# Both expert stages of a cross-attention and mixture-of-experts block: rows sorted by expert into 128-row blocks in place of every row through every expert

## The chip, the cores and the metric

The kernel runs on one core of one Trainium2 chip. The metric is device time in microseconds of that core, from the first to the last instruction and what lies around it. All arithmetic is in fp32.

## What is computed

There are 32 sequences of 56 rows of width 256, and for each a context of 1500 rows. Four stages follow each other, each added to the residual: a decayed sum of the context, 16 experts of which each row takes the best 6, attention over the masked context, and 2 experts of which each row takes the better. The reference computes every expert for every row and weights the results, zero where an expert is not chosen:

```python
# layer 0: E = 16, K = 6, MOE_D = 176
scores = jax.nn.softmax(logits.astype(jnp.float32), axis=-1)
topk_w, topk_idx = jax.lax.top_k(scores, K)
cw = cw.at[jnp.arange(T)[:, None], topk_idx].add(topk_w)
for e in range(E):
    g = h @ w_gate[e].T
    u = h @ w_up[e].T
    out = jax.nn.silu(g) * u @ w_down[e].T
    y = y + cw[:, e:e + 1].astype(x.dtype) * out
# layer 1: E = 2, FF = 1024
sel = jnp.argmax(probs, axis=-1)
...
out = jnp.einsum('etd,te->td', y, onehot * top_w)

x = x + _L0_xattn_ref(_layernorm(x, axis=-1), ctx_2048, ...)
x = x + _L0_ffn_ref(_layernorm(x, axis=-1), ...)
x = x + _L1_xattn_ref(_layernorm(x, axis=-1), ctx_2048, mask_BxS2_bk0)
x = x + _L1_ffn_ref(_layernorm(x, axis=-1), ...)
```

## The kernel before

The residual `xr` stays in SBUF as 16 tiles. A tile holds a pair of sequences, one in partitions 0 to 55, the other in 64 to 119. Four tiles are a group, and a group has 448 real rows.

The first stage streams the context through four buffers with DMAs issued by SP (`load_ctx`, L93 and L96) and adds it up on PE (L205). The layer-0 weights are loaded between these (L200). Then the small matmuls of the decayed sum follow (L239 to L273), and VectorE normalizes and adds.

The first expert stage goes over the four groups. `route0` normalizes a group, transposes it (L342), computes the gate (L357), picks the best six with `V.max` and `V.match_replace` (L403, L407), and writes the weights to DRAM, from where SP reads them back, spread over the partitions (L383, L422). `experts` takes 22 chunks of 128 hidden units. In each, the weights are the stationary operand and the group's 448 transposed rows move through the array: four matmuls for gate and up (L302), a silu on ScalarE (L307), two multiplications on VectorE (L308, L310), and two matmuls down (L315). The down matmuls of a chunk come after the gate matmuls of the next. The group ahead is routed while a group is in `experts`. `add_back` turns the result (L330) and adds it (L334), and the rows of the attention are normalized and transposed into `xnp`.

The attention goes over the 16 tiles: transposes of the context (L477), scores (L514), softmax (L530), transposes of the probabilities (L541), and their product with the context (L555). The mask is prepared on POOL (L497), and the layer-1 weights are loaded by three DMAs from POOL's queue (L458). The second expert stage has the same form as the first, with 16 chunks, and each group's output goes out by SP (L616).

The Tile framework puts in the semaphores, and its scheduler sets the order of each engine's instructions by the program's order and the buffers that are free.

Of the kernel before, what the change touches and what calls it, by code (L numbers as in the profile page):

```python
# [8 lines left out]
F32 = mybir.dt.float32  # L9
U8 = mybir.dt.uint8  # L10
AF = mybir.ActivationFunctionType
ALU = mybir.AluOpType
# [4 lines left out]
P = 128  # L17
B, S, D, T = 32, 56, 256, 1500
KD = D // P  # halves of the model width
NP = B // 2  # pairs of sequences: rows 0..55 and 64..119 of a tile  # L20
GP = 4  # pairs in a group
NG = NP // GP
TOK = 2 * S  # tokens of a pair
GT = GP * TOK  # tokens of a group
TA = 11  # context rows t = 11 p + j of the first 1408, then 92 more
# [4 lines left out]
NF0 = E0 * F0 // P  # L30
E1, F1 = 2, 1024
NF1 = E1 * F1 // P
EPS = 1e-5
BIG = 1e30
ISC = 1.0 / 16.0  # 1 / sqrt(D)
# [3 lines left out]
def xattn_ffn_kernel(  # L39
# [27 lines left out]
    rows = ctx.enter_context(tc.tile_pool(name="rows", bufs=2))  # L67
    cpool = ctx.enter_context(tc.tile_pool(name="ctx", bufs=4))
    dram = ctx.enter_context(tc.tile_pool(name="scratch", bufs=1, space=DRAM))

# [1 line left out]
    ident = const.tile([P, P], F32, name="ident")  # L72
    make_identity(nc, ident)
    flip = const.tile([P, P], F32, name="flip")  # ones where row + column = 127
    G.memset(flip, 0.0)
    G.affine_select(
        out=flip, in_=flip, compare_op=ALU.not_equal, fill=1.0,
        base=-(P - 1), pattern=[[1, P]], channel_multiplier=1,
    )
    ones = const.tile([P, P], F32, name="ones")  # L80
    G.memset(ones, 1.0)
    eps = const.tile([P, 1], F32, name="eps")
    G.memset(eps, EPS)

# [4 lines left out]
    xnp = const.tile([P, KD, NP * P], F32, name="xnp")  # normed, transposed, with pad columns  # L89
# [12 lines left out]
    def norm_scales(src, n):  # L102
        """Mean and 1 / sqrt(var + eps) of each row of n tiles."""
# [19 lines left out]
    with tc.tile_pool(name="w0", bufs=1) as w0p:  # L123
        wg0_sb = w0p.tile([P, KD, E0 * F0], F32, name="wg0_sb")
        wu0_sb = w0p.tile([P, KD, E0 * F0], F32, name="wu0_sb")
        wd0_sb = w0p.tile([P, NF0, D], F32, name="wd0_sb")
        with tc.tile_pool(name="p1", bufs=1) as p1, tc.tile_pool(
            name="p1_ps", bufs=2, space=PSUM
        ) as ps, tc.tile_pool(name="p1_acc", bufs=1, space=PSUM) as psa:
            kd = p1.tile([1, 4], F32, name="kd")  # L130
            nc.sync.dma_start(out=kd[:, 0:1], in_=decay)
            # row u of the context counts sum_{j < T - u} k^j times in the sum of the states
            # k = sigmoid(decay) by exp(-|decay|), which stays finite
# [32 lines left out]
            # count columns at place B - 1 of a row of zeros  # L166
# [25 lines left out]
            # four column groups of the array, each with a quarter of the chunks  # L192
            acc = psa.tile([P, D], F32, name="acc")
            ncq = NCH // 4
            w0_after = {12: (wg0_sb, wg0), 18: (wu0_sb, wu0), 24: (wd0_sb, wd0)}
            for b in range(B):
                c = load_ctx(b)
                if b in w0_after:
                    sb, w = w0_after[b]
                    nc.sync.dma_start(out=sb, in_=w)  # L200
# [12 lines left out]
            xn0 = p1.tile([P, NP, D], F32, name="xn0")  # L213
# [8 lines left out]
            selb = p1.tile([B, B, 64], F32, name="selb")  # L222
            V.tensor_copy(selb, ident[0:B, 0:B].unsqueeze(2).to_broadcast([B, B, 64]))
            selbf = selb.rearrange("q b s -> q (b s)")
# [44 lines left out]
            for g in range(NG):  # L269
                gs = slice(GP * g, GP * g + GP)  # L270
                for p in range(GP * g, GP * g + GP):
                    bp = ps.tile([P, 512], F32, tag="ps", name="bp")
                    PE.matmul(  # L273
                        bp[:, 0:D], lhsT=selbf[:, p * P : (p + 1) * P], rhs=m_sb,
                        start=True, stop=True,
                    )
                    V.tensor_tensor(xn0[:, p, :], xn0[:, p, :], bp[:, 0:D], ALU.add)
# [5 lines left out]
        # the first two pairs of the cross attention load during the experts  # L283
# [393 lines left out]
```

## Time and profile before

| | |
|---|---|
| time, median of two runs | 1326.16 us (1325.67 to 1326.65) |
| span of the profiled execution | 1323.2 us |
| PE busy | 1160.0 us (88%), 5104 instructions |
| VectorE, ScalarE, POOL busy | 452.5, 250.5 and 70.4 us |
| expert matmuls, lines 302 and 315 | 258.0 + 254.9 + 254.3 us of PE |
| bytes moved | 143.79 MB, mean 109 GB/s |

The profile is of one execution. PE is the matmul engine and PEld its weight loads, which overlap it. DVE is VectorE, ACT is ScalarE, POOL is GpSimd, SP issues DMAs. An fp32 matmul leaves two records in the trace. A group of instructions is named by its line, its engine and output<-input. The runs' median lies 3 us above the profiled execution's span; no time other than the span is known for that execution.

### The profile page before, as it was taken

What the parts mean: (1) busy time and instruction counts of PE and PEld (TensorE: products, weight loads), DVE (VectorE), ACT (ScalarE), POOL (GpSimd) and SP (SyncE); (2) the same over time, 40 slices, a digit from 0 to 9 for tenths busy, and PEclk for the clock granted to TensorE, in tenths of its full rate; (3) what the DMA queues carried; (4) which work ended last, traced back from release to release, by engine and by line L of the source; (5) the groups of instructions that cost most, each with busy time, mean ns of one, the idle gap of its engine ahead of it and who ended that gap; (6) DMA issues with size and microseconds to landing.
All of it is one profiled execution on the core that took longest, in us unless ns stands there. A gap on an engine that the chain in (4) does not pass through costs nothing. (4 is left out here: it accounts for less than half of the span.)

```text
span 1323.2 us, 13044 instructions
## 1 busy us (share of the span) xinstructions
PE 1160.0 (88%) x5104; PEld 623.1 (47%) x5104; DVE 452.5 (34%) x1166; ACT 250.5 (19%) x412; POOL 70.4 (5%) x81
## 2 busy tenths in 40 slices
PE   5534455899999999999999998989898999999998
PEld 3111122455555555555445555656564545555554
DVE  2400008622532442332343443433434323232322
ACT  0000000211311321121143332323322111121111
POOL 1300002100000000000021011010100000000000
PEclk9576775799999999999999999999999999999999
DMA  9999990111111111111055345352520001000000
GB/s 304 332 340 338 346 321 35 49 65 56 42 50 51 47 50 49 49 53 53 18 204 198 145 154 185 113 189 108 192 94 15 15 0 28 0 28 1 14 0 14
DMA packets 38445, 143.79 MB, mean 109 GB/s; under 512 B 5031, under 2 KB 29168, under 8 KB 29424
## 3 DMA queue, kind: packets, MB, share of 16 engines
q1 hardware_dynamic: 35122, 134.03, 28.9%
q0 software_dynamic: 432, 6.29, 1.2%
q10 hardware_dynamic: 2830, 2.64, 0.8%
q8 instruction: 40, 0.66, 0.2%
q14 instruction: 21, 0.17, 0.0%
HBM read 140.98 MB, written 1.96 MB: 108 GB/s over the span
## 5 line engine op out<-in xcount | busy, mean ns | idle before, releaser
L302 PE MATMUL gp<-xnT,wg_sb 128*128 128x448 f32 x608 | 258.0, 543 | 0.0
L302 PE MATMUL up<-xnT,wu_sb 128*128 128x448 f32 x608 | 254.9, 540 | 0.0
L315 PE MATMUL y<-hh,wd_sb 128*128 128x448 f32 x608 | 254.3, 541 | 0.0
L308 DVE TENSOR_TENSOR sg<-sg,up 128x448 f32<-128x448 f32 x152 | 94.2, 620 | 422.0 <-PE up L302 417.3
L307 ACT ACTIVATE sg<-gp 128x448 f32<-128x448 f32 x152 | 82.3, 543 | 525.5 <-PE gp L302 517.8
L315 PEld LDWEIGHTS y<-hh,wd_sb 128*128 128x128 f32 x608 | 114.0, 190 | 112.4 <-issue 105.4
L302 PEld LDWEIGHTS up<-xnT,wu_sb 128*128 128x128 f32 x608 | 114.4, 191 | 106.7 <-issue 106.7
L205 PE MATMUL acc<-ctx,cz 128*32 128x256 f32 (+1 forms) x768 | 82.3, 562 | 93.7 <-DMA ctx<-in_cx 93.4
L302 PEld LDWEIGHTS gp<-xnT,wg_sb 128*128 128x128 f32 x608 | 113.7, 191 | 101.8 <-issue 101.8
L477 PE MATMUL tp<-ident,ctx 128*128 128x128 f32 (+1 forms) x768 | 113.5, 284 | 19.9 <-DMA ctx<-in_cx 10.8
L477 PEld LDWEIGHTS tp<-ident,ctx 128*128 128x128 f32 (+1 forms) x768 | 86.0, 145 | 63.1 <-ACT cT L486 18.4
L514 PE MATMUL sp<-cT,xnp 128*64 128x512 f32 (+1 forms) x384 | 103.0, 586 | 0.8 <-DVE mx L520 0.8
L205 PEld LDWEIGHTS acc<-ctx,cz 128*32 128x32 f32 (+1 forms) x768 | 32.5, 148 | 142.2 <-DMA ctx<-in_cx 119.3
L555 PE MATMUL op<-ctx,pT 128*64 128x256 f32 (+1 forms) x768 | 99.2, 387 | 0.0
L310 DVE TENSOR_TENSOR hh<-sg,cwb 128x448 f32<-128x448 f32 x152 | 94.8, 624 | 5.7 <-DMA cwb<-cw 1.0
L486 ACT COPY cT<-tp 128x512 f32<-128x512 f32 (+1 forms) x128 | 71.7, 569 | 96.0 <-PE tp L477 93.0
L555 PEld LDWEIGHTS op<-ctx,pT 128*64 128x64 f32 (+1 forms) x768 | 55.6, 138 | 31.1 <-issue 5.7
L484 DVE COPY cT<-tp 128x512 f32<-128x512 f32 x64 | 44.1, 689 | 73.1 <-PE tp L477 73.1
L514 PEld LDWEIGHTS sp<-cT,xnp 128*64 128x64 f32 x384 | 34.1, 136 | 47.1 <-issue 43.0
L110 ACT ACTIVATE rs<-mv,eps 128x4 f32<-128x4 f32 x20 | 5.9, 297 | 242.8 <-DVE mv L109 242.7
L530 ACT ACTIVATE sc<-sc,nb 128x1500 f32<-128x1500 f32 x16 | 24.8, 1547 | 118.6 <-DVE nb L529 118.6
L497 POOL TENSOR_SCALAR mf<-mu 128x1408 f32<-128x1408 uint8 x16 | 32.7, 2045 | 257.5 <-DVE mx L520 240.4
(116 smaller groups left out, 545.4 us busy)
## 6 DMA issues: line engine op xcount, KB each, us to landing
ctx<-in_cx SPq DMA_DIRECT2D x64, 1408.0 KB
cwb<-cw SPq DMA_DIRECT2D x40, 224.0 KB
ctx<-in_cx SPq DMA_DIRECT2D x64, 92.0 KB
cwb<-cw SPq DMA_DIRECT2D x16, 196.0 KB
mu<-in_mask SPq DMA_DIRECT2D x32, 93.8 KB
wg_sb<-in_wg SPq DMA_DIRECT2D x1, 2816.0 KB
wu_sb<-in_wu SPq DMA_DIRECT2D x1, 2816.0 KB
wd_sb<-in_wd SPq DMA_DIRECT2D x1, 2816.0 KB
```

What stands on the lines that cost most here:

```text
L205: PE.matmul(acc[32 * g : 32 * g + 32, :], lhsT=cz[0:r, j, B - 1 - b : 2 * B - 1 - b], rhs=c[0:r, j, :], start=(b == 0 and m == 0), stop=(b ...
L302: PE.matmul(o, lhsT=w[:, k, i * P : (i + 1) * P], rhs=xnT[:, k, :], start=(k == 0), stop=(k == KD - 1),)
L307: A.activation(sg, gp, AF.Silu)
L308: V.tensor_tensor(sg, sg, up, ALU.mult)
L310: V.tensor_tensor(hh, sg, weight(i), ALU.mult)
L315: PE.matmul(ys[k], lhsT=wd[:, i - 1, k * P : (k + 1) * P], rhs=hh, start=(i == 1), stop=(i == nf),)
L477: PE.transpose(tp[:, jj * P : jj * P + r], c[0:r, 4 * n + jj, k * P : (k + 1) * P], ident[0:r, 0:r],)
L484: V.tensor_copy(dst, tp[:, 0 : widths[n]])
L486: A.copy(dst, tp[:, 0 : widths[n]])
L497: G.tensor_scalar(mf[:, 0:TM].rearrange("q (j p) -> q j p", p=P), mu[:, 0:TM].rearrange("q (p j) -> q j p", j=TA), -1.0, BIG, ALU.add, ALU ...
L514: PE.matmul(sp[64 * h : 64 * h + 64, 0:w], lhsT=xnp[:, k, p * P + 64 * h : p * P + 64 * h + 64], rhs=cTs[h][:, k, cols], start=(k == 0), s ...
L555: PE.matmul(op[64 * h : 64 * h + 64, :], lhsT=pT[0:r, j, 64 * h : 64 * h + 64], rhs=ctxs[2 * p + h][0:r, j, :], start=(j == 0), stop=(j == ...
```

## The change

Both expert stages are rewritten. All 16 tiles are normalized and routed at once. `places` gives each chosen pair of row and expert a place in a list that is sorted by expert, with each expert's part filled up to a multiple of 128. `clear_rows` zeroes a DRAM buffer for that list (99 blocks of 128 rows in layer 0, 15 in layer 1), `scatter_rows` writes the normalized rows there by indirect DMA, one for each tile and choice (96 and 16), and `gather_add` reads the results back by as many indirect DMAs and adds them, weighted, on VectorE.

`expert_blocks` goes over the blocks. A block's rows are read by SP, transposed, and become the stationary operand; the weights of the block's expert move. Where they stand in SBUF is read from the tile `ei` into a register of PE (`value_load`), and each matmul's address is worked out from it. In layer 0 a block is one unit of 176 hidden units; in layer 1 it has four units of 256. PE's order in this function is written out by hand: the gate of unit t, the turn of unit t - 1, the rows of the next block, the down matmuls of unit t - 2. A hidden unit's half has 88 or 128 columns, so that the down weights are kept in halves of that height.

The layer-0 weights are therefore laid out by expert in one tile `w0_sb`, loaded by `load_up0` and `load_down0` at the same three places among the context loads; the layer-1 weights are laid out in `w1_sb` by five DMAs from POOL's queue. The first stage's broadcast of its result takes two matmuls of 64 output rows for a tile in place of one of 128. `xnp`, the normalized rows and `xn0` share one buffer.

```diff
+    def gate_probs(rt, ptr, pl, xn, n, gw, ne):
+        lp = pl.tile([P, 512], F32, tag="gu", name="lp")
+        for q in range(n):
+            tp = ptr.tile([P, 512], F32, tag="tr", name="tp")
+            for k in range(KD):
+                PE.transpose(tp[:, k * P : (k + 1) * P], xn[:, q, k * P : (k + 1) * P], ident)
+            xT = rows.tile([P, KD * P], F32, tag="xT", name="xT")
+            A.copy(xT, tp[:, 0 : KD * P])
+            for k in range(KD):
+                PE.matmul(
+                    lp[:, q * ne : (q + 1) * ne], lhsT=xT[:, k * P : (k + 1) * P],
+                    rhs=gw[:, k, :], start=(k == 0), stop=(k == KD - 1),
+                )
+        lv = lp[:, 0 : n * ne].rearrange("p (q e) -> p q e", e=ne)
...
+    def places(rt, pl, sel, n, ne, kk, nb, wcols):
+        sf = sel.rearrange("p q e -> p (q e)")
+        rk = pl.tile([P, 512], F32, tag="gu", name="rk")
+        PE.matmul(rk[:, 0 : n * ne], lhsT=before, rhs=sf, start=True, stop=True)
+        tot = pl.tile([P, 512], F32, tag="gu", name="tot")
+        PE.matmul(tot[:, 0 : n * ne], lhsT=ones, rhs=sf, start=True, stop=True)
...
+        pos = rt.tile([P, n, ne], F32, name="pos")
+        V.tensor_tensor(
+            pos, rk[:, 0 : n * ne].rearrange("p (q e) -> p q e", e=ne),
+            upto.rearrange("p e q -> p q e"), ALU.add,
+        )
+        V.tensor_tensor(pos, pos, sel, ALU.mult)
+        if kk > 1:
+            top = rt.tile([P, n, 8], F32, name="top")
+            for q in range(n):
+                V.max(out=top[:, q, :], in_=pos[:, q, :])
+            top = top[:, :, 0:kk]
+        else:
+            top = rt.tile([P, n, 1], F32, name="top")
+            V.tensor_reduce(top, pos, AX.X, ALU.add)
...
+        to = rt.tile([P, n, kk], I32, name="to")
+        V.tensor_scalar(to, top, pad, None, ALU.add)
+        of = rt.tile([P, n, kk], I32, name="of")
+        V.tensor_scalar(of, top, -1.0, 0.0, ALU.add, ALU.max)
...
+        ep = pl.tile([P, 512], F32, tag="gu", name="ep")
+        PE.transpose(ep[0:1, 0:P], ex, ident)
+        ei = rt.tile([1, P], I32, name="ei")
+        V.tensor_copy(ei, ep[0:1, 0:P])
+        return to, of, ei
+    def clear_rows(name, nb):
+        xs = dram.tile([nb * P, D], F32, name=f"xs{name}")
+        nc.scalar.dma_start(
+            out=xs.rearrange("(p j) d -> p j d", j=nb),
+            in_=zero.unsqueeze(1).to_broadcast([P, nb, D]),
+        )
+        return xs
+    def scatter_rows(name, xs, xn, to, n, kk, nb):
+        for q in range(n):
+            for k in range(kk):
+                i = G.indirect_dma_start(
+                    out=xs, out_offset=bass.IndirectOffsetOnAxis(ap=to[:, q, k : k + 1], axis=0),
+                    in_=xn[:, q, :], in_offset=None,
+                    bounds_check=nb * P - 1, oob_is_err=False,
+                )
+                tc.declare_no_dep(i.ins, group=f"xs{name}", reason="no two rows have one place")
+                tc.add_to_no_dep_group(f"xs{name}", i.ins)
+    def expert_blocks(name, nb, xs, ei, w, nq, f, wk, ptr, pgu, pht, py):
+        fp = f // nq
+        h = fp // 2
+        doff = 2 * KD * fp
+        piece = doff + 2 * D
+        ys = dram.tile([nb * P, D], F32, name=f"ys{name}")
+        units = [(i, u) for i in range(nb) for u in range(nq)]
+        xT, at, hs, hT, y = {}, {}, {}, {}, {}
+        def rows_in(i):
+            xb = wk.tile([P, D], F32, tag="xb", name="xb")
+            nc.sync.dma_start(out=xb, in_=xs[i * P : (i + 1) * P, :])
+            tp = ptr.tile([P, 512], F32, tag="tr", name="tp")
+            for k in range(KD):
+                PE.transpose(tp[:, k * P : (k + 1) * P], xb[:, k * P : (k + 1) * P], ident)
+            xT[i] = wk.tile([P, KD * P], F32, tag="xbT", name="xbT")
+            A.copy(xT[i], tp[:, 0 : KD * P])
+        def gate_up(i, u):
+            if u == 0:
+                at[i] = PE.value_load(
+                    ei[0:1, i : i + 1], min_val=0, max_val=w.shape[1] - nq * piece
+                )
+            gu = pgu.tile([P, 512], F32, tag="gu", name="gu")
+            for k in range(KD):
+                PE.matmul(
+                    gu[:, 0 : 2 * fp], lhsT=xT[i][:, k * P : (k + 1) * P],
+                    rhs=w[:, bass.ds(at[i] + (u * piece + k * 2 * fp), 2 * fp)],
+                    start=(k == 0), stop=(k == KD - 1),
+                )
+            sg = wk.tile([P, fp], F32, tag="sg", name="sg")
+            A.activation(sg, gu[:, 0:fp], AF.Silu)
+            hs[i, u] = wk.tile([P, fp], F32, tag="hs", name="hs")
+            V.tensor_tensor(hs[i, u], sg, gu[:, fp : 2 * fp], ALU.mult)
+        def turn(i, u):
+            tp = pht.tile([P, 512], F32, tag="ht", name="tp")
+            a = hs.pop((i, u))
+            for c in range(2):
+                PE.transpose(tp[0:h, c * P : (c + 1) * P], a[:, c * h : (c + 1) * h], ident)
+            hT[i, u] = wk.tile([h, 2 * P], F32, tag="hT", name="hT")
+            V.tensor_copy(hT[i, u], tp[0:h, 0 : 2 * P])
+        def down(i, u):
+            if u == 0:
+                y[i] = py.tile([P, 512], F32, tag="y", name="y")
+            a = hT.pop((i, u))
+            for c in range(2):
+                PE.matmul(
+                    y[i][:, 0:D], lhsT=a[:, c * P : (c + 1) * P],
+                    rhs=w[0:h, bass.ds(at[i] + (u * piece + doff + c * D), D)],
+                    start=(u == 0 and c == 0), stop=(u == nq - 1 and c == 1),
+                )
+            if u == nq - 1:
+                yb = wk.tile([P, D], F32, tag="yb", name="yb")
+                A.copy(yb, y.pop(i)[:, 0:D])
+                nc.sync.dma_start(out=ys[i * P : (i + 1) * P, :], in_=yb)
+        with tc.manual_schedule(engines={mybir.EngineType.PE}):
+            rows_in(0)
+            for t in range(len(units) + 2):
+                if t < len(units):
+                    gate_up(*units[t])
+                if 0 <= t - 1 < len(units):
+                    turn(*units[t - 1])
+                if t < len(units) and units[t][1] == 0 and units[t][0] + 1 < nb:
+                    rows_in(units[t][0] + 1)
+                if t >= 2:
+                    down(*units[t - 2])
+        return ys
...
+    def gather_add(gp, tiles, ys, of, ws, kk):
+        for q, p in enumerate(tiles):
+            for k in range(kk):
+                yg = gp.tile([P, D], F32, tag="yg", name="yg")
+                G.indirect_dma_start(
+                    out=yg, out_offset=None, in_=ys,
+                    in_offset=bass.IndirectOffsetOnAxis(ap=of[:, q, k : k + 1], axis=0),
+                )
+                V.scalar_tensor_tensor(
+                    xr[:, p, :], yg, ws[:, q, k : k + 1], xr[:, p, :], ALU.mult, ALU.add
+                )
...
+        def load_up0(m, w):
+            for k in range(KD):
+                nc.sync.dma_start(
+                    out=w0_sb[:, :, (2 * k + m) * F0 : (2 * k + m + 1) * F0],
+                    in_=w[:, k, :].rearrange("p (e f) -> p e f", f=F0),
+                )
+        def load_down0(w):
+            for e in range(E0):
+                for c in range(2):
+                    r = 0
+                    while r < H0:
+                        f = e * F0 + c * H0 + r
+                        n = min(H0 - r, P - f % P)
+                        o = 2 * KD * F0 + c * D
+                        nc.sync.dma_start(
+                            out=w0_sb[r : r + n, e, o : o + D],
+                            in_=w[f % P : f % P + n, f // P, :],
+                        )
+                        r += n
...
-        def experts(g, pools, nf, ne, xnT, wg, wu, wd, weight):
...
-                            PE.matmul(
-                                o, lhsT=w[:, k, i * P : (i + 1) * P], rhs=xnT[:, k, :],
-                                start=(k == 0), stop=(k == KD - 1),
-                            )
...
-                    A.activation(sg, gp, AF.Silu)
-                    V.tensor_tensor(sg, sg, up, ALU.mult)
-                    hh = wk.tile([P, GT], F32, tag="hh", name="hh")
-                    V.tensor_tensor(hh, sg, weight(i), ALU.mult)
...
-                    for k in range(KD):
-                        PE.matmul(
-                            ys[k], lhsT=wd[:, i - 1, k * P : (k + 1) * P], rhs=hh,
-                            start=(i == 1), stop=(i == nf),
-                        )
-            return ys
...
-            routed = route0(0)
-            for g in range(NG):
-                ahead = route0(g + 1) if g + 1 < NG else None
-                xnT, cd = routed
-                ys = experts(
-                    g, (wk, pgu, py), NF0, E0, xnT, wg0_sb, wu0_sb, wd0_sb, weight0(cd)
-                )
-                add_back(g, ys, yT, pm)
...
+            xs = clear_rows("0", NB0)
+            xn = normed_rows(allrows, tiles)
+            pr = gate_probs(rt, ptr, pgu, xn, NP, gw0_sb, E0)
+            m8 = rt.tile([P, NP, 8], F32, name="m8")
+            rp = rt.tile([P, NP, E0 + 2], F32, name="rp")
+            for q in range(NP):
+                V.max(out=m8[:, q, :], in_=pr[:, q, 0:E0])
+            V.memset(m8[:, :, K0:8], -1.0)
...
+            sel = rt.tile([P, NP, E0], F32, name="sel")
+            V.tensor_scalar(sel, rp[:, :, 0:E0], -1.5, valid, ALU.is_lt, ALU.mult)
+            to, of, ei = places(rt, pgu, sel, NP, E0, K0, NB0, W0)
+            scatter_rows("0", xs, xn, to, NP, K0, NB0)
...
+            ys = expert_blocks(
+                "0", NB0, xs, ei, w0_sb.rearrange("p e w -> p (e w)"), 1, F0,
+                wk, ptr, pgu, pht, py,
+            )
+            gather_add(gp, tiles, ys, of, ws, K0)
...
-    for sb, w in ((wg1_sb, wg1), (wu1_sb, wu1), (wd1_sb, wd1)):
-        nc.gpsimd.dma_start(out=sb, in_=w)
+    w1_sb = w1p.tile([P, E1 * NQ1, W1], F32, name="w1_sb")
+    fq = F1 // NQ1
+    for m, w in ((0, wg1), (1, wu1)):
+        for k in range(KD):
+            nc.gpsimd.dma_start(
+                out=w1_sb[:, :, (2 * k + m) * fq : (2 * k + m + 1) * fq],
+                in_=w[:, k, :].rearrange("p (e f) -> p e f", f=fq),
+            )
+    nc.gpsimd.dma_start(
+        out=w1_sb[:, :, 2 * KD * fq : W1].rearrange("p e (c d) -> p e c d", d=D),
+        in_=wd1.rearrange("p (e c) d -> p e c d", c=2),
+    )
...
-        routed = route1(0)
-        for g in range(NG):
-            ahead = route1(g + 1) if g + 1 < NG else None
-            xnT, ws = routed
-            ys = experts(
-                g, (wk, pgu, py), NF1, E1, xnT, wg1_sb, wu1_sb, wd1_sb,
-                lambda i: ws[i // (F1 // P)],
-            )
-            add_back(g, ys, yT, pm)
+        xs = clear_rows("1", NB1)
+        xn = normed_rows(allrows, tiles)
+        pr = gate_probs(rt, ptr, pgu, xn, NP, gw1_sb, E1)
...
+        to, of, ei = places(rt, pgu, sel, NP, E1, K1, NB1, NQ1 * W1)
+        scatter_rows("1", xs, xn, to, NP, K1, NB1)
+        ys = expert_blocks(
+            "1", NB1, xs, ei, w1_sb.rearrange("p e w -> p (e w)"), NQ1, F1,
+            wk, ptr, pgu, pht, py,
+        )
+        gather_add(gp, tiles, ys, of, ws, K1)
```

## The prediction

> **What bounds the kernel now.** I read the table of stages first, because the average over the span hides that the stages have different limits. I cut it at the instructions that end a stage: the last context matmul (L205), the first expert matmul (L302), the last expert matmul of layer 0 (L315), the last attention matmul (L555). The columns are the length, then busy time on PE, PEld, DVE, ACT and POOL, then the granted clock, the DMA share and GB/s.
>
> ```profile
> 0.00:193.50 193.50, 89.28 (x798) 39.38 (x798) 24.48 (x84) 3.96 (x7) 17.16 (x28) 0.71 0.93 330
> 193.50:242.90 49.40, 26.08 (x72) 16.20 (x73) 38.87 (x120) 1.78 (x6) 13.52 (x17) 0.50 0.16 60
> 242.90:658.61 415.71, 415.34 (x1195) 213.40 (x1195) 145.24 (x361) 81.95 (x135) 0.00 (x0) 1.00 0.16 49
> 658.61:1009.45 350.84, 322.42 (x2129) 195.57 (x2128) 142.31 (x378) 109.92 (x177) 39.74 (x36) 0.98 0.41 150
> 1009.45:1323.20 313.75, 306.86 (x912) 158.52 (x912) 101.56 (x225) 52.88 (x87) 0.00 (x0) 1.00 0.04 12
> ```
>
> Stage one is a transfer (DMA share 0.93, PE under half). Stage two is VectorE. The two expert stages (415.7 and 313.8 us) are PE without a hole, at full clock, with routing hidden under the previous group's matmuls. So fewer columns through PE would shorten them, and anything put in front of or behind them, with PE waiting, is paid in full.
>
> The prices of PE come from the chain of work (first line, start and length) and from PE's timeline (second). The first shows four records, which are two fp32 matmuls of 448 columns, in 1.50 us: 1.68 ns a column. The second shows 16 transposes in 2.50 us: 0.16 us each.
>
> ```profile
> 1035.16 1.50 PE up L302 x4
> 678.19 2.50 PE L477 MATMUL tp<-ident,ctx 128*128 128x128 f32 x16 [0.24 <-ACT cT L486]
> ```
>
> The DMA queues give two packet prices.
>
> ```profile
> q1 hardware_dynamic: 35122, 134.03, 28.9%
> q10 hardware_dynamic: 2830, 2.64, 0.8%
> ```
>
> Busy engine time is share x 16 x 1323 us. For q1, with 3.8 KB a packet on average, 134.03 MB in 6118 us is 21.9 GB/s an engine, 350 GB/s for 16. For q10, with 0.9 KB a packet, 2.64 MB in 169 us is 250 GB/s for 16.
>
> No indirect DMA is in the trace. The nearest rows are POOL's own plain loads, each of which covers 128 partition rows; the issue by SP of a 128-row transfer (L93: 0.34 us median); and the shortest trip to memory, L383, whose landing lets L602 start 1.2 us after its issue began.
>
> ```profile
> 659.01 0.74 POOL L458 DMA_DIRECT2D wg_sb<-in_wg  x1 [422.37 <-PE y L315]
> 659.76 0.54 POOL L458 DMA_DIRECT2D wu_sb<-in_wu  x1
> 660.29 0.53 POOL L458 DMA_DIRECT2D wd_sb<-in_wd  x1
> 1021.04 0.25 SPq L383 DMA_DIRECT2D cw<-cT  x1
> 1022.24 0.83 SPq L602 DMA_DIRECT2D cwb<-cw  x2
> ```
>
> **The change, part by part.**
>
> *Stage one.* The cleared buffers are 12,672 + 1,920 rows of 1 KB, 14.9 MB, issued near the start by ACT, while the DMA share is already 0.93. At 350 GB/s that is 43 us, at 250 GB/s 60 us. The 8.65 MB of layer-0 weights now arrive in pieces of 704 B and 1 KB: 35 us at 250 GB/s instead of 25 at 350, so +10 at most. The down weights become dozens of SP issues of 8 to 88 rows, at 0.34 us each, ahead of the last eight context loads; SP's waits for buffers cover them, and with that cover gone some 50 x 0.34 = 17 us would show. The idle DMA share, 0.07 x 193.5 = 13 us, may absorb some. Ends +30 and +70; I take **+55**.
>
> *Routing of layer 0.* Before, experts begin when one group is routed; now all 16 tiles must be. Eight more tiles of normalization, 0.97 us each on DVE (0.40 + 0.16 + 0.41), are 8 us; the last tile's transposes, copy and gate matmul 2 us. Then one serial chain on DVE, priced by these rows (minimum/median/maximum ns):
>
> ```profile
> L403 DVE MAX8 m<-pr x16: 158/160/178, 251.0 to 471.3; 112x8 f32<-112x16 f32 x16
> L407 DVE MATCH_VALUE_LOAD rp<-m,pr x16: 80/82/92, 251.5 to 472.1; 112x8 f32 x16
> L407 DVE MATCH_REPLACE8 rp<-m,pr x16: 160/161/164, 251.6 to 472.1; 112x18 f32<-112x18 f32 x16
> ```
>
> That is 32 maxima x 0.16 = 5.1, 16 replacements x 0.24 = 3.9, about ten operations of 256 columns x 0.42 = 4.2, a dozen small ones x 0.2 = 2.4, a table load 1.3 with its exponential, two matmuls at the halved clock of stage two, and handovers: 24 us. **+34**, ends +20 and +50.
>
> *Scatter of layer 0.* 96 indirect DMAs of 128 rows on POOL. The built kernel's lists show eight completion semaphores in rotation, so eight are in flight, and the first block's read waits for all eight, hence for every scatter. PE's next instruction is that block's transpose: nothing hides this phase. Price c of one: below, 0.34 (SP's row) or 0.53 (POOL's plain row); above, 0.74 + 1.2 = 1.94, as if each waited for its landing. An indirect one resembles POOL's plain one, but has to fetch 128 offsets and address each row alone, so I take twice POOL's row, **c = 1.25**. 96 x 1.25 + 3 for the last landing = **+123**.
>
> The Trainium skill ("DMA: Bandwidth & Descriptors", section "Anatomy of one DMA — SWDGE (gpsimd) path") speaks against this change: about 2 us fixed plus bytes over 436 GB/s for each DMA. By it 128 KB cost an estimated 2.3 us, and were they serial, the sum below would be some 235 us higher; no row here shows an indirect one, and POOL's plain issues follow each other after 0.54 us.
>
> *Blocks of layer 0.* 99 blocks, whatever the routing. Each has two matmuls of 352 columns (704 x 1.68 = 1.18 us), two of 256 (0.86) and four transposes (0.64): 2.68 us. New is a register load from SBUF on PE ahead of each block and address arithmetic ahead of each matmul. Below it costs nothing, since the down matmuls queued ahead last 0.86 us; above, a trip to memory, 1.2 us. I take 0.42, so **b = 3.1** (ends 2.7 and 3.9). Per block ACT needs some 1.0 us (two copies of 0.37, a silu of about 0.27), DVE 0.7, SP two issues: hidden under 3.1, while three buffers keep reads ahead. 99 x 3.1 + 5 to fill = 312, in place of 415.7: **-104**.
>
> The Trainium skill ("DMA: Bandwidth & Descriptors", section "Latency and other measured facts") gives a floor of about 600 ns for such a register load; if all of it showed, the estimate for a block would be 3.28 us, 21 us more in all.
>
> *Gather of layer 0.* 96 x 1.25 = 120, plus 10 for the last block's write, first landing, and the last tiles' norm. On POOL two of the five loads of layer-1 weights stand among them; they now have 1,024 rows each, by POOL's row 0.5 us if rows cost nothing and 4.3 if time goes with rows: +8. PE's next instructions are the 32 transposes that need these rows, and all attention is queued behind them. **+138**.
>
> *Attention* itself is unchanged, but its first mask is queued on POOL behind the last gather and three more weight loads (13 us) and PE can run only a few tiles ahead: **+10**, ends 0 and +20.
>
> *Layer 1.* Routing now starts after attention instead of running beside it: 22. Scatter 16 x 1.25 + 3 = 23. 60 units of 1,024 + 512 columns and two transposes (1.72 + 0.86 + 0.32 = 2.90) are 174, and 15 blocks' row transposes and register loads 11, fill 4: 189. Gather 24, output 5. Together 263 in place of 313.8: **-51**.
>
> *Sum.* 55 + 34 + 123 - 104 + 138 + 10 - 51 = +205. The profiled span of 1323.2 becomes 1528; the median of the runs, 1326.16, lies 3 above the span, so **1531 us**.
>
> **The rivals.**
>
> *The issue is nearly free.* The mechanism is POOL's price for an indirect DMA. The sum is zero at c = 1.25 - 205/224 = 0.33. With SP's row, 0.34, it is 1531 - 224 x 0.91 = **1327**, not slower. For it: hardware issues 128 rows at that price, and eight in flight hide landings. Against it: POOL's plain issues take 0.53 at the least, and they need no offsets.
>
> *Each indirect DMA costs a round trip* (c = 1.94): 1531 + 224 x 0.69 = **1686**. For it: descriptors are built from data in memory. Against it: eight semaphores in rotation.
>
> *The register load drains PE* (b = 3.9): 114 blocks x 0.8 = +91, **1622**. For it: it stands between matmuls in PE's own queue. Against it: 0.86 us of matmuls are queued ahead of it.
>
> *The change saves less work than it says*: 99 + 15 blocks are sized for the worst routing, not the real one. That is in the sum already: even so PE's columns fall from 236,544 to 120,384 in layer 0 (without transposes), so this alone doesn't turn it.
>
> **How the numbers follow.** Forecast 0.60; free issue 0.10; round trip 0.15; register load 0.15. The range: c from 0.75 to 1.9 moves the sum by -112 and +146, b from 2.9 to 3.3 by 23 either way, stage one by 20. Taken together, 1390 to 1690, which holds the last two rivals. About 2% is what a measurement of this kernel can tell from no change. Faster by more needs c below 0.21, or c at POOL's plain row with both other terms at their low ends: 0.05. Within 2%: 0.05. Slower: 0.90.
>
> **What would show it.** Right: two stretches of some 120 us in layer 0 with POOL busy and PE idle; a block every 3.1 us; the last context matmul near 250 us; the first block near 400. The sum is wrong if the scatter lasts under 50 us or over 180, or a block needs more than 4 us.

## The result, and the profile after

The changed kernel took **1467.6 us** (median; 1467.4 to 1467.9) against 1326.2: ratio 1.108, 95% interval 1.104 to 1.111. It is slower. The forecast was 1531, its range 1390 to 1690.

First comes the table of stages of the changed kernel, cut at the same places as before and also around the two stretches in which PE stands still. The columns are again the length, then busy time (and count) on PE, PEld, DVE, ACT and POOL, then the granted clock (PE's clock as a share of full speed), the DMA share and GB/s.

```profile
0.00:255.68 255.68, 94.12 (x798) 40.70 (x798) 23.33 (x79) 3.96 (x7) 20.39 (x31) 0.64 0.89 308
255.68:337.13 81.45, 42.79 (x184) 28.53 (x183) 57.94 (x236) 9.83 (x26) 13.45 (x20) 0.52 0.10 37
337.13:463.29 126.16, 0.00 (x0) 0.00 (x0) 4.39 (x11) 0.00 (x0) 93.68 (x96) 0.50 0.25 89
463.29:716.00 252.71, 250.50 (x1188) 187.29 (x1188) 65.83 (x198) 105.99 (x297) 0.00 (x0) 0.99 0.32 102
716.00:861.65 145.65, 10.15 (x32) 4.70 (x32) 60.32 (x148) 8.81 (x22) 100.33 (x103) 0.51 0.41 122
861.65:1215.86 354.21, 324.52 (x2135) 199.36 (x2135) 138.69 (x366) 108.02 (x175) 33.95 (x32) 0.97 0.37 135
1215.86:1466.00 250.14, 188.24 (x711) 118.12 (x709) 60.18 (x173) 42.39 (x106) 31.03 (x32) 0.86 0.12 39
```

The third row has no PE instruction at all, the fifth 32. Between them stand the 99 blocks, with PE busy for 250.5 of 252.7 us: the work saved is real, and it is paid for in front and behind. Laid beside the forecast's terms:

| stage | before, us | after, us | measured | forecast |
|---|---|---|---|---|
| context sum | 193.5 | 255.7 | +62 | +55 |
| routing, layer 0 | 49.4 | 81.5 | +32 | +34 |
| scatter, layer 0 | - | 126.2 | +126 | +123 |
| blocks, layer 0 | 415.7 | 252.7 | -163 | -104 |
| gather, layer 0 | - | 145.7 | +146 | +138 |
| attention | 350.8 | 354.2 | +3 | +10 |
| layer 1 | 313.8 | 250.1 | -64 | -51 |
| sum | 1323.2 | 1466.0 | +143 | +205 |

POOL's timeline shows the price that was in no row of before. The columns are start, length, the instruction, and in brackets the idle time ahead of it and what ended it. The first lines are scatters, the last two gathers.

```profile
342.56 0.97 POOL L248 DMA_INDIRECT xs<-xn,to  x1 [0.30 <-issue]
343.84 0.97 POOL L248 DMA_INDIRECT xs<-xn,to  x1 [0.30 <-issue]
...
458.80 0.97 POOL L248 DMA_INDIRECT xs<-xn,to  x1 [0.30 <-issue]
...
726.74 0.95 POOL L333 DMA_INDIRECT yg<-ys,of  x1 [0.30 <-issue]
727.99 0.94 POOL L333 DMA_INDIRECT yg<-ys,of  x1 [0.30 <-issue]
```

From one to the next it is 1.28 us for a scatter and 1.25 for a gather of 128 rows of 1 KB: 0.97 or 0.95 of POOL's own time and 0.30 that waits for nothing the profile shows. No landing ends those waits. The section "DMA Instruction — SWDGE (GPSIMD)" of the Trainium skill's page "Perfetto Trace Analysis" says that such a record ends when the descriptors are written, not when the data have moved. The trace fits that: the last scatter's record ends at 459.8, the first block's read is issued at 461.3, and PE starts at 463.3.

The next lines are PE's timeline of one block in steady state, with the line of the following block, and the register load's record (min/median/max ns, first and last start).

```profile
477.24 1.35 PE L282 MATMUL gu<-w_sb,xbT 128*128 x4
478.42 0.38 PE L296 MATMUL tp<-ident,hs 128*88 128x128 f32 x2
478.64 0.38 PE L271 MATMUL tp<-ident,xb 128*128 128x128 f32 x2
478.86 1.03 PE L305 MATMUL y<-w_sb,hT 88*128 x4
479.72 1.35 PE L282 MATMUL gu<-w_sb,xbT 128*128 x4
...
L277 PEldq TENSOR_LOAD <-ei x114: 295/300/492, 463.9 to 1419.2; - x114
```

A block takes 479.72 - 477.24 = 2.48 us. The register load lasts 0.30 us on PE's queue, and there is no hole in front of the matmuls that use it. Two transposes are 0.22 us (478.42 to 478.64).

### The profile page after: what moved, and what is told of

Its sections match the earlier page's. It is cut to its first block, busy times and chain, and to the rows that moved or that the text cites. A ratio compares the mean times of both kernels' runs of the same rounds, so it can differ in the third digit from the quotient of the medians.

```text
span 1466.0 us, 15363 instructions
## 1 busy us (share of the span) xinstructions
PE 910.3 (62%) x5044; PEld 578.7 (39%) x5044; DVE 410.7 (28%) x1210; ACT 279.0 (19%) x633; POOL 292.8 (20%) x314
## 4 chain that ended last, share of the span: by engine, by line
PE 48%; issue 21%; DMA 16%; DVE 6%; another core or an unknown queue 4%; SPq 2%; ACT 1%; POOL 1%; ACTq 0%; DVEq 0%; POOLq 0%
PE gu L282 15%; DMA ctx<-in_cx 13%; PE y L305 9%; PE tp L631 7%; PE op L709 6%; PE sp L668 3%; DVE xr L337 3%; PE tp L296 2%; DMA yg<-ys,of 2%; PE tp L271 2%; PE tp L695 2%; SPq L360 1%; PE acc L452 1%; DMA w_sb<-in_wd 1%
## 5 line engine op out<-in xcount | busy, mean ns | idle before, releaser
L282 PE MATMUL gu<-w_sb,xbT 128*128 x636 | 251.3, 517 | 2.7 <-issue 1.5
L305 PE MATMUL y<-w_sb,hT 88*128 (+1 forms) x636 | 163.3, 379 | 0.0
L333 POOL DMA_INDIRECT yg<-ys,of x112 | 108.9, 972 | 226.7 <-DMA ys<-yb 181.7
L298 DVE COPY hT<-tp 88x256 f32<-88x256 f32 (+1 forms) x159 | 67.1, 422 | 302.0 <-PE tp L296 298.9
L282 PEld LDWEIGHTS gu<-w_sb,xbT 128*128 128x128 f32 x636 | 121.4, 192 | 64.3 <-issue 31.9
L631 PE MATMUL tp<-ident,ctx 128*128 128x128 f32 (+1 forms) x768 | 113.6, 286 | 21.5 <-DMA ctx<-in_cx 12.9
L248 POOL DMA_INDIRECT xs<-xn,to x112 | 109.4, 976 | 73.9 <-DVE of L224 40.4
L305 PEld LDWEIGHTS y<-w_sb,hT 88*128 88x128 f32 (+1 forms) x636 | 108.2, 190 | 8.6
L290 DVE TENSOR_TENSOR hs<-sg,gu 128x176 f32<-128x176 f32 (+1 forms) x159 | 56.6, 356 | 157.7 <-ACT sg L288 157.7
L288 ACT ACTIVATE sg<-gu 128x176 f32<-128x176 f32 (+1 forms) x159 | 54.5, 343 | 206.5 <-PE gu L282 203.4
L337 DVE SCALAR_TENSOR_TENSOR xr<-yg,ws,xr 128x256 f32<-128x256 f32 x112 | 53.0, 484 | 91.7 <-DMA yg<-ys,of 51.1
```

Of the source, the lines that this page charges most:

```text
L248: i = G.indirect_dma_start(out=xs, out_offset=bass.IndirectOffsetOnAxis(ap=to[:, q, k : k + 1], axis=0), in_=xn[:, q, :], in_offset=None, ...
L282: PE.matmul(gu[:, 0 : 2 * fp], lhsT=xT[i][:, k * P : (k + 1) * P], rhs=w[:, bass.ds(at[i] + (u * piece + k * 2 * fp), 2 * fp)], start=(k = ...
L298: V.tensor_copy(hT[i, u], tp[0:h, 0 : 2 * P])
L305: PE.matmul(y[i][:, 0:D], lhsT=a[:, c * P : (c + 1) * P], rhs=w[0:h, bass.ds(at[i] + (u * piece + doff + c * D), D)], start=(u == 0 and c ...
L333: G.indirect_dma_start(out=yg, out_offset=None, in_=ys, in_offset=bass.IndirectOffsetOnAxis(ap=of[:, q, k : k + 1], axis=0),)
L337: V.scalar_tensor_tensor(xr[:, p, :], yg, ws[:, q, k : k + 1], xr[:, p, :], ALU.mult, ALU.add)
```

## The experiments

The working theory after the traces: (1) stage one's end, scatter and gather stand one behind the other, each paid in full by POOL's issue price or the transfers; (2) a block costs its matmuls and nothing else. The rivals: something in the blocks still waits for the register; part of scatter or gather is covered; or the cost of stage one is not the clearing.

**The register load: static weight places.** The output is not the routing's, since block i takes the weights of a fixed expert.

```diff
-                at[i] = PE.value_load(
-                    ei[0:1, i : i + 1], min_val=0, max_val=w.shape[1] - nq * piece
-                )
+                at[i] = (i * (w.shape[1] // (nq * piece)) // nb) * nq * piece
...
```

> The changed kernel with each block's weights at a fixed place (block i takes expert i*16/99, or i*2/15), so that PE loads no register and works out no address; which rows meet which expert is therefore not the routing's. Theory: the register load (0.30 us in the trace, 114 times) and the address arithmetic run while PE's queued matmuls drain, so the blocks of layer 0 already stand at PE's own pace of 2.49 us: the time stays within 4 us of 1467.6. Rival: the load stands in PE's stream and a block shrinks by 0.3 us or more: 114 x 0.3 = 34 us less, 1433 or below.

Measured 1467.0, ratio 1.107 (1.103 to 1.110), the same as with the load. The register load costs nothing here, and the rival falls.

**The scatter: one row set of six.**

```diff
-            scatter_rows("0", xs, xn, to, NP, K0, NB0)
+            scatter_rows("0", xs, xn, to, NP, 1, NB0)
```

> The first expert stage scatters only the first of its six row sets (16 of 96 indirect stores); the other rows of its blocks keep the cleared zeros, the blocks, weights and gathers are as in the changed kernel. Theory (stage one's end, the scatter and the blocks stand one behind the other, and the scatter is paid issue by issue on GpSimd): 80 stores fewer at the 1.28 us between two of them in the profile of the changed kernel (0.97 busy, 0.30 between) take 102 us away: 1468 - 102 = 1366, range 1358 to 1374. Rival (part of the scatter runs beside something that needs its time anyway, such as the clearing's last transfers or the weights): 30 to 70 us less, 1398 to 1438.

Measured 1363.1, ratio 1.032 (1.029 to 1.036). Against 1.108 that is 0.075 x 1326 = 100 us for 80 scatters, 1.25 us each. PE's timeline of this run has the first block at 364.4, where the scatter began at 340.3.

```profile
364.37 0.69 PE L271 MATMUL tp<-ident,xb 128*128 128x128 f32 x2 [27.35 <-DMA xb<-xs]
```

Nothing covers the scatter, as the theory says.

**The gather: moved into the attention, tile by tile.** All norms, transposes and gathers of layer 0's results are done tile by tile, one or two tiles ahead of its scores, not for all 16 ahead of the attention; `tile_rows` is one tile's norm, its two transposes and their copy.

```diff
...
-            gather_add(gp, tiles, ys, of, ws, K0)
...
+            for p in range(NP):
...
+                attend(p, sc, mx3)
+                if p + 1 < NP:
+                    tile_rows(p + 1)
+                if p + 2 < NP:
+                    gather_add(gp0, [p + 2], ys0, of0, ws0, K0)
...
```

> The changed kernel with the gathers of layer 0 moved: the six gathers, the norm and the transposes of a tile are issued tile by tile, two tiles ahead of the attention of that tile, in POOL's order written by hand (gathers of a tile, then the next mask). Theory: the 146 us between the last block and the attention are POOL issuing one after the other with PE waiting only for its place in the queue; a tile needs 6 x 1.28 = 7.7 us of POOL against 22 us of attention, so all but the first tile hides: scores start some 20 us after the last block instead of 148, and the time falls by 120 to 128, to 1343. Rival: in the attention the gathers, the 96 additions on VectorE and two table loads a tile on ScalarE stand in the way, 3 us a tile: about 1390.

Measured 1403.3, ratio 1.059 (1.056 to 1.062): 64 us less and not 124. The stretch between the blocks and the first scores fell from 146 us to 35 (713.6 to 748.5), 15 more than expected, and the attention grew from 354 us to 401:

```profile
748.50:1149.70 401.20, 330.45 (x2115) 197.60 (x2114) 182.66 (x508) 137.69 (x217) 114.46 (x116) 0.94 0.42 142
```

DVE carries 44 us more than in the attention's row above, ACT 30, POOL 81; PE only 6. So 47 of the 111 us that had gone from in front of the attention came back inside it: PE's waits there rose from 29 us to 70, most of them ended by ACT and DVE. ScalarE changed between the square root's and the exponential's tables at every tile, which is the first thing to suspect, since its table loads, 6 and 4 in the changed kernel, had risen to these (lines of the costliest groups: count, then busy time, mean ns and idle time ahead):

```profile
L128 ACT ACT_TABLE_LOAD x16 | 20.5, 1283 | 96.2 <-DMA xr<-in_x 95.9
L669 ACT ACT_TABLE_LOAD x14 | 18.0, 1283 | 0.2
```

**The table loads: norms in groups of 1, 1, 2, 4, 4 and 4 tiles.** The buffer pools are also smaller: one buffer for the normed rows, five for gathered rows.

```diff
-                if p + 1 < NP:
-                    tile_rows(p + 1)
-                if p + 2 < NP:
-                    gather_add(gp0, [p + 2], ys0, of0, ws0, K0)
+                if p + 1 in groups:
+                    tile_rows(groups[p + 1])
+                gather_add(gp0, ahead.get(p, []), ys0, of0, ws0, K0)
...
```

> As the run with the gathers inside attention (1403 us), but the norms taken over groups of 1, 1, 2, 4, 4 and 4 tiles, each group ahead of its first tile, so that ScalarE changes between the square root's and the exponential's tables 6 times in place of 16; the gathers are issued earlier, up to four tiles ahead. Theory (the table changes, 1.28 us each way in that run's profile, stand in each tile pair's chain): 10 pairs at 2.57 us are 26 us less, 1372 to 1385. Rival (the tile's chain is set by the gathers' adds and TensorE's transposes, the table loads lie beside them): 1395 to 1410.

Measured 1402.2, ratio 1.061 (1.056 to 1.066): no change, though 16 table loads are gone.

```profile
L128 ACT ACT_TABLE_LOAD x8 | 10.3, 1283 | 95.1 <-DMA xr<-in_x 95.0
L669 ACT ACT_TABLE_LOAD x6 | 7.7, 1283 | 6.5 <-DVE mx L663 6.4
```

The theory of the table loads falls as a forecast. The scores start at 751.8 and the attention still takes 397 us. PE's waits in it that ACT had ended did fall, from 45 us to 10, but those ended by DVE rose from 22 to 34 and those for context loads from 1 to 9. The smaller pools changed in the same run, so what the tables alone would give isn't shown. Which of the remaining additions (the adds and norms on DVE, the masks behind the gathers on POOL, the smaller pools) sets the tile's pace stays open.

**The clearing: 13 MB behind the context stream.** The zeros are made from the finished rows, so that the transfer cannot start early.

```diff
...
-            xs = clear_rows("0", NB0)
+            zl = rt.tile([P, D], F32, name="zl")
+            V.tensor_scalar(zl, xr[:, 0, :], 0.0, None, ALU.mult)
+            xs = clear_rows("0", NB0, zl)
```

> The changed kernel with one edit: the zeros for the 13 MB buffer of layer 0 come from a tile that is written when the first tiles of the residual are ready, so that the clearing DMA starts after the context stream instead of beside it. Theory: the 62 us by which stage one grew are mostly the bytes of that clearing, 13.0 MB at 250 to 350 GB/s = 37 to 52 us, and the DMA engines are idle enough in the 81 us before the first scatter to take them: 1416 to 1431 us, last context matmul at 204 to 219 us. Rival: stage one grew by the 704-byte pieces and the 52 small issues of the layer-0 weights: then at most 15 us go, 1452 or more.

Measured 1430.9, ratio 1.080 (1.076 to 1.085), 37 us less. The last context matmul ended at 222.8 in place of 255.7, so the clearing is 33 of the 62 us. 29 are left, and the sight of 52 small transfers issued by SP one after the other suggested the next run. These are the issues' record in the changed kernel and the stretch that they take there, then two stretches of the DMA engines while they last in the late-clearing run.

```profile
L360 SPq DMA_DIRECT2D w_sb<-in_wd x52: 278/356/2293, 181.6 to 215.8; - x52
181.60:216.20 34.60, 11.15 (x96) 3.95 (x96) 0.00 (x0) 0.00 (x0) 0.00 (x0) 0.50 0.50 159
```

```profile
155.00:160.00 5.00, 2.31 (x24) 0.75 (x21) 0.00 (x0) 0.00 (x0) 0.00 (x0) 0.50 0.35 120
160.00:165.00 5.00, 2.54 (x36) 0.97 (x31) 0.00 (x0) 0.00 (x0) 0.00 (x0) 0.83 0.25 81
```

With a DMA share of 0.25 to 0.35 the engines starve: the context loads stand behind the issues.

**The issues: the down weights in one transfer of 88 rows**, on top of the late clearing.

```diff
...
-                        nc.sync.dma_start(
-                            out=w0_sb[r : r + n, e, o : o + D],
-                            in_=w[f % P : f % P + n, f // P, :],
-                        )
...
+            nc.sync.dma_start(out=w0_sb[0:H0, :, 2 * KD * F0 : W0], in_=w)
...
```

> As the run with the late clearing (1431 us), and the down weights of the first expert stage laid out ahead of the launch as 88 rows, so that one transfer brings them in place of 52 small ones. Theory (SyncE's queue spends 34 us, from 181.6 to 215.8 in the changed kernel's profile, on issuing the 52 down transfers, and the context loads queued behind them start late): 15 to 29 us less, the last context matmul at 194 to 208 in place of 222.8, 1402 to 1416. Rival (the issues are covered by SyncE's waits for free context buffers, as the prediction had it, and the bytes of the weights alone make the rest of the delay): within 5 us, 1426 to 1436.

Measured 1434.0, ratio 1.087 (1.083 to 1.091): nothing gained; the last context matmul ended at 220.5. The starving is gone, but another limit took its place. Three stretches of this run, after its issue at 147.6, and SP's issue of the next context load (start and length):

```profile
156.00:159.00 3.00, 0.17 (x4) 0.17 (x8) 0.00 (x0) 0.00 (x0) 0.00 (x0) 0.50 0.73 184
159.00:162.00 3.00, 3.00 (x24) 0.99 (x20) 0.00 (x0) 0.00 (x0) 0.00 (x0) 0.50 0.71 141
162.00:165.00 3.00, 0.02 (x1) 0.00 (x0) 0.00 (x0) 0.00 (x0) 0.00 (x0) 0.98 0.70 156
150.46 19.31 SPq L109 DMA_DIRECT2D ctx<-in_cx  x1
```

The share stands at 0.70 to 0.73 and the rate at 141 to 184 GB/s, where stage one of the kernel before ran at 330. The next context load's issue took 19.31 us, and nothing else of the stream was issued meanwhile.

**The pieces: all weights of the stage in SBUF's order**, as rows of 24 and 29 KB to 88 partitions and pieces of 2.8 KB to 40, in three pairs of transfers.

```diff
...
+            nc.sync.dma_start(out=w0_sb[0:H0, e0:e1, :], in_=wg0[:, e0:e1, :])
+            nc.sync.dma_start(out=w0_sb[H0:P, e0:e1, 0:UP0], in_=wu0[:, e0:e1, :])
...
```

> As the run with the late clearing, and the first expert stage's weights laid out ahead of the launch in the order in which they stand in SBUF, so that three pairs of transfers with long rows bring them in place of 4 transfers in pieces of 704 bytes and 52 of 1 KB. In that run the last context matmul ended at 222.8, and the run with only the down weights in one transfer left it at 220.5, so the issues are not it. Theory (the small pieces of the weights take the DMA engines' time: 285 GB/s in place of 347 beside the up weights, 146 to 209 beside the down weights): the last context matmul ends at 200 to 208, 15 to 22 us less than the late clearing's 1431, 1409 to 1416 where the kernel before takes 1325 (ratio 1.063 to 1.069). Rival (the layout of the rows does not matter, the number of bytes or the place of the loads in the queue does): 218 to 223, within 5 us of 1431, ratio 1.077 to 1.084.

Measured 1458.0, ratio 1.099 (1.096 to 1.101): 27 us more than the late clearing, and outside what either theory allowed. The last context matmul ended at 257.7. The whole of stage one in the run with the late clearing, in the one with one transfer, and in this one:

```profile
0.00:222.75 222.75, 92.34 (x798) 40.22 (x798) 22.67 (x79) 3.96 (x7) 20.46 (x31) 0.64 0.87 296
0.00:220.50 220.50, 91.47 (x798) 39.94 (x798) 22.66 (x79) 3.96 (x7) 20.46 (x31) 0.65 0.91 299
0.00:257.70 257.70, 95.66 (x798) 41.68 (x798) 22.66 (x79) 3.96 (x7) 20.46 (x31) 0.62 0.87 257
```

The share is 0.87 here as with the late clearing. What fell is the rate of the engines while they work: GB/s over share is 340, 329 and here 295, against 355 in the kernel before. The sizes and times of the packets in the traces say it too. Packets of 24,320 bytes to 88 partitions took a mean of 1.74 us here, 14.0 GB/s an engine. The 704-byte pieces of the late-clearing run moved at 16.6, and the kernel before brought its weights to 128 partitions in packets of 22,528 bytes at 23.9. So pieces of 704 bytes are slower than long rows to 128 partitions, and long rows to 88 partitions are slower still.

What the two rearrangements share, and the kernel before does not, is a transfer to 88 (and 40) partitions in place of 128. The Trainium skill's page "DMA: Bandwidth & Descriptors", section "Why a DMA increments its semaphore by 16 and not by 1", has a rule for that: a transfer is spread over the largest number of engines up to 16 that divides its row counts, so 88 rows go to 11 engines and 40 to 10. By the page 11 of 16 is an estimated share of 0.69. The plateau of 0.70 to 0.73 fits it, and so do the packets of the run with one transfer: from 144 to 150 us 16 to 18 are in flight at any time, from 153 to 168 mostly 11 to 13, with a mean of 11.4. That 11 engines carried this transfer is shown; that the row count alone decides it is not, as no run changed only that. Nor does it say why the busy engines were slower, which is the larger part of the 35 us by which stage one grew against the late clearing. That cause stays open.

**Both clearings late, with these weights.**

```diff
...
+            xs1 = clear_rows("1", NB1, zl)
...
```

> As the run with the weights laid out, and the second clearing (1.9 MB, issued at 8.5 us in the runs so far) also behind the context stream. Theory (each cleared MB costs the stream about 3 to 4 us, as stage one ended at 194.4 in place of 202.9 in the version with only the second stage rewritten): 6 to 9 us less than the run with the weights laid out, the last context matmul at 193 to 200, with which the whole of stage one's 62 us is accounted for; 1401 to 1409. Rival (the stream has room for 1.9 MB): the same as the run with the weights laid out within 3 us.

Measured 1481.6, ratio 1.118 (1.115 to 1.120): 24 us more, where 6 to 9 less was expected. Stage one did end earlier, at 252.1 in place of 257.7. But routing grew from 81.7 us to 113.6, and ACT's timeline says why:

```profile
294.24 34.06 ACTq L239 DMA_DIRECT2D xs<-zl  x2
328.34 0.67 ACT L126 ACTIVATE rs<-mv,eps 128x4 f32<-128x4 f32 x3 [39.62 <-issue]
```

The second issue, with 13 MB already queued, held ACT's queue for 33 us, and the norms of the routing stood behind it. With one clearing the issue took 0.53 us. So the moved transfer brought a wait to the engine that issues it.

**Only the second expert stage rewritten**, the first and the attention as in the kernel before; in place of the second stage's groups:

```diff
+            xs = clear_rows("1", NB1, zero)
...
+        scatter_rows("1", xs, xn, to, NP, K1, NB1)
+        ys = expert_blocks(
...
+        gather_add(gp, tiles, ys, of, ws, K1)
```

> The kernel before, with the second expert stage alone rewritten as in the change (15 blocks in 4 units, 16 scatters, 16 gathers, 2 MB cleared at the start); the first expert stage stays as it was. Theory: the stages' costs add up one by one. Layer 1 was 63.6 us shorter in the changed kernel, and clearing 2 MB at 250 to 350 GB/s costs 6 to 8 us in stage one: 1326.2 - 63.6 + 7 = 1270 us. Rival: part of those 63.6 us was work that only the new first stage takes out of the way of the attention and of layer 1; then 1290 or more.

Measured 1270.7, ratio 0.959 (0.957 to 0.962): it beats both kernels, and the theory that the stages' costs add up had given 1270. Its clearing is 1,920 rows, 2.0 MB, beside the context stream (the 2.4 MB of two expectations below is a miscount), and its scatter and gather are 16 issues each.

**The same with its clearing late**, in the first expert stage:

```diff
-            xs = clear_rows("1", NB1, zero)
+            zl = yp.tile([P, D], F32, name="zl")
+            G.memset(zl, 0.0)
+            xs1 = clear_rows("1", NB1, zl)
```

> As the version with only the second expert stage rewritten (1270.7 us), but its clearing of 18 blocks (2.4 MB) issued in the first expert stage and not at the start beside the context stream. Theory (the clearing's bytes delay the context stream: 33 us for 13 MB of zeros moved away is 2.5 us per MB): 5 to 8 us less, 1262 to 1266. Rival (2.4 MB fit into the gaps of the context stream): within 2 us of 1270.

Measured 1264.5, ratio 0.959 (0.955 to 0.964), on another chip than the run before it. Its profile had the last context matmul at 194.4 in place of 202.8, but the ratio had not moved, so both were run once more on one chip.

> The kernel before with only the second expert stage rewritten, once more, beside the next run on one chip. Both theories: ratio 0.956 to 0.963.

> The same with its clearing of 2.4 MB issued behind the context stream, which ended stage one at 194.4 in place of 202.9 in the profiles, while the measured ratios of two separate chips did not differ. Theory (stage one's gain reaches the end): 6 to 10 us less than the run before it on the same chip. Rival (the end does not move, something else is later instead): within 3 us of it.

Early clearing: 1270.4, ratio 0.958 (0.957 to 0.960). Late: **1265.3, ratio 0.954 (0.953 to 0.956)**. The gain is real, 5 us, a little under the 6 to 10 expected; the profiled spans are 9 us apart (1265.2 and 1256.2). This is the fastest version that ran.

## Why the prediction was right, and where it was off

The direction and the mechanism held: two stretches of over 120 us with POOL busy and PE idle, and the sum of seven terms within its range. Point by point:

- *The price of an indirect DMA*, the term on which everything hung, was taken as 1.25 us from twice POOL's plain row. It measured 1.28 and 1.25, and the run with one scatter of six showed it paid in full. The factor of two had no row behind it: that it came out within 0.03 us is luck, while the bounds of 0.34 and 1.94 around it were reasoned. Both rivals that lived on this price fall. A free issue (0.34) is excluded by the rows. The round trip (1.94) is excluded by the wait in the rows, 0.30, which no landing ends. The 2 us fixed for each DMA, which the prediction held against the change from the Trainium skill ("DMA: Bandwidth & Descriptors", section "Anatomy of one DMA — SWDGE (gpsimd) path"), is not what a stream of them costs here: one follows the other after 1.28 us.
- *The blocks* were the mis-sized term: 3.1 us forecast, 2.48 measured, 99 x 0.6 = 60 of the 63 us by which the sum was too high. The step that failed is "I take 0.42" for the register load. The argument against a cost was in the prediction itself (0.86 us of matmuls queued ahead) and should have been followed: taking the load of 0.30 us away changed nothing (1467.0 against 1467.6). The rest is the transposes, priced at 0.16 us each from the context's transposes and measured 0.11 in a block. The floor of about 600 ns that the Trainium skill gives (same page, section "Latency and other measured facts") is twice the 0.30 us of the trace, and neither showed in the time. The rival in which the register load drains PE falls with the same run.
- *Layer 1* was 13 us better than forecast, for the same reasons: a unit of 1,024 + 512 columns came every 2.80 us and not 2.90 (60 x 0.1 = 6), and the register loads of its 15 blocks don't show.
- *Stage one*: +62 for +55, inside its ends. The clearing's share was right in kind and smaller (33 us for 13 MB, 2.5 us per MB). The 13 MB were issued at 99.9 us and not near the start. "SP's waits for buffers cover them" is wrong: over the 52 issues in the changed kernel (181.6 to 216.2) the DMA share averaged 0.50, which is an estimated 17 us of lost transfer time, the very 17 that the prediction gave for a missing cover. With 33 us for the first clearing and 6 to 9 for the second (the end of stage one in the pairs of runs that moved it), about 20 of the 62 us belong to how the weights come in, and the idle engines account for most of them. One transfer in place of the 52 raised the stage's share from 0.87 to 0.91 and gained 2 us only, because the rate of the busy engines fell (329 for 340), for a cause not shown.
- *Gather*: +146 for +138. The 96 gathers took 131.8 us of it (720.4 to 852.2) and not 120, because some waited longer than 0.30 us (8 us more together, most of it ended by DVE), and a plain load of 1,024 rows stood among them. There was one such load, not two, and it took 0.95 us, near the low end of the 0.5 to 4.3 given. Ahead of them stand 4.4 us, behind them 9.5.
- *Routing and attention*: +32 for +34, and +3 for +10. The mask behind the gathers cost little.
- *A slip*: "the first block near 400" contradicts the prediction's own sum (193.5 + 55 + 49.4 + 34 + 123 = 455). It was at 463.

What would have to change for the first stage: 96 scatters and 96 gathers are 243 us of POOL for 163 us saved on PE. Even the late clearing and the gathers inside the attention together would leave an estimated 1467.6 - 37 - 64 = 1367, worked out from the two runs as if they add up. In the second stage 32 issues, 40 us, stand against a halving of PE's columns, and that stage alone wins.

## What to carry to other kernels

Price a sorted mixture of experts by rows moved as well as by work saved: one indirect DMA of 128 rows cost 1.25 to 1.28 us of POOL here in each direction, so a row with six experts pays twelve shares of that and a row with one expert two. Here the stage in which each row has one expert and much work was worth the rewriting, and the one with six was not. A wait in an engine's own queue need not show when queued work ahead of it lasts longer: here 0.86 us of matmuls stood ahead of a load of 0.30.

## What the runs showed of the hardware that was not expected

- A register load from SBUF on PE's queue took 0.30 us and could not be seen in the time.
- POOL's plain DMA of 1,024 rows took 0.95 us, against 0.53 for 128 rows: eight times the rows, less than twice the time.
- An issue onto ACT's queue behind 13 MB took 33 us, and ACT's arithmetic waited for it.
- Rearranging 8.65 MB of weights into longer rows, on 88 and 40 partitions, made the stage 35 us slower (222.8 to 257.7): the share of busy engines stayed at 0.87, their rate fell from 340 to 295 GB/s.
- A transfer to 88 partitions ran with 11 to 13 packets in flight, where the loads to 128 partitions had 16 to 18.
